# One written list for the slots around each later image's beginning, and 1/std turned on VectorE

## The chip, the cores and the metric

The kernel runs on one core of one Trainium2 chip. The metric is the device time of one execution in microseconds (us), the median over the runs of a kernel. Engines are TensorE (PE, with its weight loads as PEld), VectorE (DVE), ScalarE (ACT), GpSimd (POOL) and SyncE (SP), which issues most of the DMAs. Each has its own queue, in the order in which the program issues; they meet through semaphores.

## The reference, cut to what matters

Four images of 128 channels by 128 x 128 pixels go through two layers, all in float32. Each layer first normalises its input over groups of four channels of an image (`_gn`), so nothing of a layer can start on an image before that image's statistics are complete.

```python
# layer 0: token mixing, per pixel over the 128 channels
def _block(x, ...):
    t = _ln(t, ln0_g, ln0_b)
    y1 = _ln(t, ln1_g, ln1_b)
    t = t + einsum('btc,oc->bto', sigmoid(y1) * y1, W_out)
    y2 = _ln(t, ln2_g, ln2_b)
    wht = einsum('btc,oc->bto', y2, W_whiten)
    k = square(relu(einsum('btc,hc->bth', wht, W_key)))      # 512 hidden
    kv = einsum('bth,ch->btc', k, W_value)
    r = sigmoid(einsum('btc,oc->bto', wht, W_recep))
    return t + r * kv
x = x + block(_gn(x)) + transposed(block(transposed(_gn(x))))   # the same twice
# layer 1: 3x3 convolution, 128 to 128 channels, expert 0 alone, bias,
# and a squeeze-and-excite factor per output channel
v = _gn(x); avg = v.mean(axis=(2, 3))
out = conv3x3(v, weight[0]) + bias_e[0]
x = x + out * sigmoid(relu(avg @ se_w1.T) @ se_w2.T)
```

Both halves of layer 0 work pixel by pixel, so they are the same and are computed once and doubled.

## The kernel before, in words

**Tiles.** An image has 32 chunks of 512 pixels (four rows); two chunks are a pair `g`, so an image has 16 pairs (`NP`) and the run has 64. A block of 16 rows (`NBLK` = 8 per image) stays in SBUF from its load to the store of its result.

**Layer 0 on a pair.** Short words name its operations; a digit in a word is the chunk of the pair, and in `pk`, `re`, `sq` and `kv` a second digit is one of four hidden quarters. ScalarE normalises by group (`u`), TensorE turns the chunk so that pixels lie on partitions (`Tu`), VectorE takes statistics over channels (`bn`), GpSimd makes 1/std and the shift out of them (`nb`, with a power in L642), ScalarE applies them (`t`), GpSimd applies gain and shift (`g`, `b`). A second normalisation (`z1`, its transposes `Tz`), `silu`, the product `att` and the sum `T` follow; then the third statistics (`bn2`, `nb2`).

**1/std of the third normalisation.** It is not applied to the pixels' rows. It is turned, stored and spread: `Tr` (L698) is a TensorE transpose of the 128 x 8 tile `rs` into a bank "rt", `rc` (L702) copies that to SBUF on VectorE, `W` (L706) stores the 8 x 128 rows to DRAM from SyncE, `R` (L711) reads each chunk's 512 values back, spread over 128 partitions, and `cp` (L715) multiplies the turned chunk `tt` with it into `y`, the input of the key products `pk` (L726) and of the receptance `pr` (L744). `re`, `sq`, `kv` (L753), `th`, `q`, `x` and `S` finish the layer; `bx` takes statistics for layer 1.

**Layer 1 on a block.** A transformed (Winograd-like, along the rows) convolution: VectorE makes six mixtures `v0` to `v5` of the rows, TensorE multiplies each with its transformed weights `u` (`c0` to `c5`, three matmuls of some 512 columns each, L791 to L793), and VectorE and ScalarE put the results together (`e1`, `e3`, `a` to `d`, `y0` to `y3`). It runs four slots behind layer 0 and reaches across images without a break.

**Order.** The lists of words are the order of issue, for all engines at once. In the steady part the list ORDER is one slot: slot `s` runs each word `op:k` on pair `s - k`; conv words take turns, even and odd slots doing half a block each. FILL and HANDOVER are lists written out for the first slots and for the stretch where layer 1 of image 0 starts; END is that of the last four slots.

**The two chains.** When an image begins, two chains of small steps have to be run. `input_norm(b)` makes the group statistics of image `b` out of the statistics of its input (`xs`, read from DRAM a second time by SyncE, `fetch` and `in`): an aggregate, two tiny matmuls `pm` (L401) and `pv` (L409), a power on GpSimd. `conv_setup(b)` does the same for layer 1 (L484 to L508), computes the squeeze-and-excite factor by three more matmuls (L512, L518, L521) and two tanh, and scales the six transformed weights with it on VectorE (`scale`, `add_identity`, L535 and L539). It reads the weights anew from DRAM, three of them only when the previous image's last block has used theirs. Both are generators; a `yield` ends a step. In the slots of ORDER a step is run after every third word:

```python
if s % NP == done and b > 1:
    chains.append(conv_setup(b - 1))
...
    if n % 3 == 2:
        for chain in chains:
            next(chain, None)
```

so `input_norm` of an image lies in the slot before the image begins and `conv_setup` in the slot `done` = 3 after it. HANDOVER and END have the steps of `conv_setup` as words of their own, `*`.

Of the kernel before, what the change touches and what calls it, by code (L numbers as in the profile page):

```python
# [13 lines left out]
P = 128  # L14
# [29 lines left out]
    in1:20 u1:4 in0:20 z10:1 g1:2 bn00:3 fetch:21 z11:1 bn01:3 nb2:0 b0:2 Tr:0 Tz10:1 rc:0  # L44
    nb0:3 W:0 silu0:1 Tz11:1 att0:1 silu1:1 in1:21 bn10:2 R0:0 att1:1 in0:21 b1:2 t0:3 T0:1
# [4 lines left out]
    att0:2 sq02:0 pw2:1 sq03:0 kv02:0 T0:2 th0:0 nb2:1 nb1:3 Tr:1 Tz11:2 t1:4 rc:1 kv03:0  # L50
    sq10:0 W:1 pk13:0 q0:0 silu1:2 Tu1:5 in0:23 re12:0 att1:2 bn20:2 t0:4 R0:1 pr1:0 g1:4
    bn01:5 kv10:0 sq11:0 R1:1 x10:0 T1:2 Tu0:5 sq12:0 kv11:0 z10:3 bn00:5 tt1:1 tt0:1 nb0:5
    kv12:0 th1:0 cp0:1 re13:0 pr0:1 sq13:0 cp1:1 pk03:1 z11:3 S1:1 pk00:1 bn21:2 th0:1
    kv13:0 g0:4 S0:1 re00:1 Tz11:3 bx0:0 pk01:1 re03:1 b1:4 sq00:1 silu1:3 pk02:1 b0:4
    bn11:4 re01:1 Tz10:3 att1:3 re02:1 nb2:2 bn10:4 silu0:3 pk12:1 q1:0 pk10:1 re12:1 T1:3
    att0:3 sq03:1 bn21:3 sq01:1 kv00:1 nb1:4 re10:1 Tr:2 pk11:1 sq02:1 rc:2 sq10:1 W:2
    pk13:1 re11:1 T0:3 kv01:1 sq11:1 bn20:3 t1:5 kv02:1 x11:0 R0:2 kv03:1 sq12:1 nb2:3 tt0:2
    q0:1 re13:1 R1:2 pr1:1 bx1:0 t0:5 kv10:1 S0:2 kv11:1 sq13:1 kv12:1 x10:1 z10:4 cp0:2
    tt1:2 pk01:2 g0:5 S1:2 th1:1 pk00:2 cp1:2 re01:2 g1:5 Tr:3 pk03:2 re00:2 rc:3 kv13:1
    sq00:2 re03:2 in1:23 pk02:2 q1:1 pk10:2 bx0:1 x11:1 kv00:2 Tz10:4 bx1:1  # L60
# [11 lines left out]
    x10:4 cp1:3 Tr:2 pk02:3 rc:2 q1:4 bx0:4 t1:0 x11:4 g1:0 z10:1 bx1:4 pk10:3 kv00:3 Tz10:1  # L72
    g0:0 re03:3
# [13 lines left out]
    Tu1:18 kv12:13 re01:14 pk12:14 bn01:18 re03:14 Tu0:18 u0:19 pk02:14 bn00:18 g0:17 Tr:15  # L87
# [10 lines left out]
    Tr:16 att0:17 rc:16 x10:15 bn11:18 W:16 pk12:15 re11:15 bx1:13 tt0:16 nb1:18 sq11:15  # L98
    pk13:15 T0:17 u0:20 bx0:15 t1:19 R0:16 Tu0:20 bn20:17 kv10:15 kv11:15 R1:16 re12:15
    S0:16 re13:15 att1:17 bn00:20 g0:19 sq12:15 sq13:15 kv12:15 g1:19 * kv13:15 cp0:16 u1:20  # L100
    * b1:19 u1:21 Tu1:20 q1:15 pk01:16 z10:18 bn01:20 x11:15 pk00:16 nb0:20 re01:16 bx1:15
    Tz10:18 pr0:16 re00:16 T1:17 sq00:16 * tt1:16 silu0:18 bn21:17 * th0:16 att0:18 sq01:16
    cp1:16 nb2:17 t0:20 * pk10:16 p:0 bn11:19 pk11:16 t1:20 pk03:16 S1:16 * T0:18 b0:19
    Tr:17 re10:16 kv00:16 * rc:17 re03:16 in0:32 kv01:16 W:17 g1:20 re11:16 bn10:19 Tu1:21
    z11:18 pk02:16 b1:20 bn01:21 pk12:16 R0:17 re02:16 nb1:19 * Tz11:18 bn11:20 sq02:16
    tt0:17 u0:21 kv02:16 fetch:33 S0:17 sq03:16 bn20:18 * Tu0:21 re12:16 R1:17 pk13:16 *
    sq10:16 bn00:21 kv03:16 g0:20 silu1:18 cp0:17 pr1:16 z11:19 q0:16 b0:20 att1:18 sq11:16
    kv10:16 * T1:18 sq12:16 nb0:21 tt1:17 * in0:33 re13:16 kv11:16 in1:33 th1:16 pk00:17
    S1:17 fetch:34 sq13:16 * z10:19 kv12:16 * bn10:20 * * re00:17 kv13:16 bn21:18 nb1:20 *
    Tz10:19 * t0:21 cp1:17 pk01:17 in0:34 Tz11:19 pk02:17 re01:17 * * silu1:19 pk10:17 * q:0  # L110
    silu0:19 nb2:18 pr0:17 q2:0 sq00:17 att1:19 * re10:17 att0:19 t1:21 T1:19 pk03:17 q1:16
    x10:16 Tr:18 sq01:17 kv00:17 rc:18 bn21:19 re02:17 W:18 g1:21 kv01:17 sq02:17 T0:19
    pk12:17 th0:17 g0:21 in1:34 re03:17 kv02:17 bn20:19 x11:16 R0:18 sq03:17 tt0:18 z10:20
    pk11:17 S0:18 b0:21 kv03:17 * bx0:16 sq10:17 pk13:17 nb2:19 q0:17 re12:17 Tz10:20 *
    re11:17 kv10:17 z11:20 cp0:18 pr1:17 * pk00:18 * sq11:17 b1:21 bn10:21 Tz11:20 re13:17
    kv11:17 silu0:20 p2:0 pk02:18 re00:18 v3:0 Tr:19 silu1:20 pk01:18 v1:0 th1:17 rc:19
    att1:20 bn11:21 W:19 re02:18 att0:20 * re01:18 nb1:21 T1:20 c1:0 sq01:18 bn21:20 u0:22
    R1:19 T0:20 u1:22 bn20:20 R0:19 tt0:19 e1:0 Tu1:22 tt1:18 x10:17 sq02:18 bn01:22 c3:0
    R1:18 z11:21 nb2:20 * fetch:35 sq13:17 sq12:17 Tu0:22 pr0:18 sq00:18 bn00:22 e3:0
    pk03:18 th0:18 v4:0 nb0:22 kv12:17 * cp1:18 kv13:17 re03:18 cp0:19 pk11:18 q1:17 pk10:18  # L120
    in0:35 re11:18 in1:35 c4:0 re10:18 x11:17 fetch:36 t1:22 v0a:0 sq10:18 kv00:18 g1:22 c:0
    sq03:18 kv01:18 S1:18 t0:22 S0:19 pk12:18 d:0 pk13:18 g0:22 re12:18 in0:36 kv02:18
    z10:21 * kv03:18 b1:22 in1:36 sq11:18 pr1:18 fetch:37 q0:18 sq12:18 Tz10:21 bx1:16
    x10:18 re13:18 kv10:18 th1:18 pk00:19 v5a:0 silu0:21 Tz11:21 re00:19 v2:0 pk01:19
    silu1:21 q:1 kv11:18 b0:22 sq13:18 att1:21 re01:19 tt1:19 sq00:19 T1:21 c2:0 in0:37
    in1:37 bn21:21 pk03:19 S1:19 Tr:20 kv12:18 cp1:19 re03:19 rc:20 kv13:18 a:0 W:20 pk10:19
    q1:18 pk11:19 x11:18 re10:19 att0:21 sq01:19 R0:20 re11:19 pk12:19 T0:21 sq10:19 R1:20
    pk02:19 bn20:21 re12:19 kv00:19 v5b:0 nb2:21 fetch:38 kv01:19 v0b:0 re02:19 bn10:22
    pr0:19 sq02:19 sq11:19 kv02:19 th0:19 tt0:20 sq03:19 pr1:19 cp0:20 sq12:19 pk13:19 S0:20
    th1:19 b:0 tt1:20 re13:19 kv03:19 bx0:17 pk02:20 q0:19 tt0:21 bn11:22 x10:19 re02:20  # L130
    pk00:20 sq13:19 cp1:20 kv10:19 nb1:22 * pk03:20 re00:20 S1:20 kv11:19 S0:21 y1:0 sq00:20
    kv12:19 bx1:18 pk10:20 d8:0 c5:0 bx1:17 re03:20 sq02:20 kv13:19 sq03:20 re10:20 pk11:20
    q1:19 pk01:20 y2:0 re11:20 in0:38 x11:19 kv00:20 re01:20 pr0:20 sq11:20 ca:0 sq01:20
    pk12:20 y3:0 z10:22 p:1 kv01:20 in1:38 Tr:21 kv02:20 th0:20 rc:21 W:21 kv03:20 re12:20
    c0:0 sq10:20 q0:20 x10:20 R0:21 bx0:20 pk13:20 R1:21 bx0:19 kv10:20 re13:20 pr1:20
    sq12:20 fetch:39 sq13:20 kv11:20 th1:20 cp0:21 kv12:20 y0:0 kv13:20 q1:20 pk00:21 bx1:19
    in1:39 in0:39 bx0:18
# [9 lines left out]
    y0:-5 cp1:5 pk02:5 u0:2 c5:-5 sq03:5 bx1:6 Tr:4 re02:5 S1:5 g1:3 b1:3 rc:4 y3:-5 b0:3  # L147
    bn11:3 bn10:3 kv01:5 Tu1:2 sq02:5 pk10:5 nb1:3 bn01:2 re10:5 Tu0:2 sq10:5 pk11:5 q:-4
    v1:-4 W:4 pk13:5 kv02:5 tt0:4 re11:5 pr1:5 re13:5 kv03:5 th1:5 c1:-4 z10:3 bn00:2 z11:3
    v2:-4 R0:4 Tz10:3 q0:5 cp0:4 q2:-4 pk12:5 silu0:3 nb0:2 pk00:4 re12:5 x10:5 e1:-4 v5a:-4  # L150
    v3:-4 S0:4 R1:4 v0a:-4 t1:2 t0:2 v0b:-4 g1:2 kv10:5 att0:3 Tz11:3 T0:3 pr0:4 g0:2 sq11:5
    silu1:3 re00:4 load c3:-4 sq13:5 sq12:5 kv11:5 u1:1 att1:3 b0:2 bn10:2 sq00:4 pk02:4
    b1:2 kv12:5 bn11:2 tt1:4 kv13:5 nb1:2 T1:3 e3:-4 Tu1:1 c2:-4 u0:1 th0:4 re02:4 S1:4
    bn21:3 bn20:3 u0:0 q1:5 a:-4 z10:2 b:-4 pk01:4 cp1:4 Tu0:1 pk03:4 kv00:4 bx0:5 re01:4
    nb2:3 pk10:4 Tr:3 v4:-4 c4:-4 re03:4 re10:4 sq10:4 z11:2 bn00:1 sq01:4 v5b:-4 Tz10:2
    pk12:4 silu0:2 sq02:4 sq03:4 bn01:1 rc:3 Tz11:2 kv01:4 c:-4 d:-4 pk11:4 kv02:4 re12:4
    tt0:3 u1:0 pk13:4 W:3 R0:3 y2:-4 x11:5 ca:-4 nb0:1 sq12:4 kv03:4 S0:3 y1:-4 t1:1 silu1:2
    g1:1 b1:1 R1:3 re13:4 q0:4 c0:-4 att0:2 cp0:3 bn11:1 t0:1 re11:4 sq11:4 att1:2 T0:2 T1:2
    Tu0:0 pr1:4 kv10:4 g0:1 p:-3 bn21:2 pk02:3 th1:4 pk00:3 b0:1 bn20:2 sq13:4 x10:4 nb2:2
    re00:3 q:-3 re02:3 kv11:4 Tu1:0 kv12:4 bn10:1 pk01:3 pr0:3 y0:-4 nb1:1 tt1:3 re01:3  # L160
    cp1:3 th0:3 S1:3 sq01:3 bn01:0 p2:-3 q2:-3 kv13:4 Tr:2 pk03:3 pk11:3 d8:-4 rc:2 sq02:3
    sq00:3 bn00:0 re03:3 nb0:0 W:2 z10:1 c5:-4 q1:4 pk13:3 tt0:2 re11:3 pk10:3 v1:-3 S0:2
    kv00:3 y3:-4 v3:-3 kv01:3 v0a:-3 re13:3 re10:3 x11:4 pr1:3 z11:1 kv02:3 pk12:3 R0:2 t1:0
    c1:-3 th1:3 re12:3 cp0:2 g1:0 Tz10:1 pk00:2 sq11:3 pk01:2 Tz11:1 sq03:3 v4:-3 kv03:3
    silu0:1 q0:3 sq10:3 R1:2 e1:-3 v2:-3 t0:0 silu1:1 att0:1 re00:2 v0b:-3 g0:0 c3:-3 b1:0
    tt1:2 T0:1 att1:1 pk02:2 kv10:3 bn20:1 sq13:3 S1:2 kv11:3 e3:-3 re01:2 sq12:3 re02:2
    T1:1 bn11:0 b0:0 sq01:2 kv12:3 kv13:3 bn21:1 pk03:2 re03:2 sq03:2 sq02:2 x10:3 bn10:0
# [47 lines left out]
def conv_preact_kernel(  # L215
# [863 lines left out]
```

## Time and profile before

| | |
|---|---|
| median of 3 runs | 1893.07 us (1892.37 to 1893.11) |
| profiled execution | 1896.06 us, span 1894.3 us, mean granted TensorE clock 0.993 |
| busy in the span | TensorE 1818.5 us, VectorE 1353.5, ScalarE 1276.4, GpSimd 1158.6 |
| `pk` L726 and `kv` L753 | 1024 matmul records each, mean 598 and 593 ns |
| `rt` L698 | 64 matmuls, 64 weight loads |
| `rrow` L702 | 64 copies on VectorE, mean 275 ns |
| `rs` L642, the power on GpSimd | 192, mean 1650 ns |
| `rd` stores L706, `R` loads L711 | 64 of 4 KB, 128 of 256 KB (spread) |

A float32 matmul leaves two records where its columns are streamed twice, a transpose one. Matmuls are pipelined: the duration of a record is longer than the step from its start to the start of the next, and the step is what TensorE's time is made of. A wait line names who waited, for whom, the total in us, how often, and the longest. A timeline line gives start and length in us, the engine, the line, and in brackets the idle time before it with what ended it.

### The profile page before, as it was taken

What the parts mean: (1) busy time and instruction counts of PE and PEld (TensorE: products, weight loads), DVE (VectorE), ACT (ScalarE), POOL (GpSimd) and SP (SyncE); (2) the same over time, 40 slices, a digit from 0 to 9 for tenths busy, and PEclk for the clock granted to TensorE, in tenths of its full rate; (3) what the DMA queues carried; (4) which work ended last, traced back from release to release, by engine and by line L of the source; (5) the groups of instructions that cost most, each with busy time, mean ns of one, the idle gap of its engine ahead of it and who ended that gap; (6) DMA issues with size and microseconds to landing.
All of it is one profiled execution on the core that took longest, in us unless ns stands there. A gap on an engine that the chain in (4) does not pass through costs nothing.

```text
span 1894.3 us, 21662 instructions
## 1 busy us (share of the span) xinstructions
PE 1818.5 (96%) x6160; PEld 946.7 (50%) x6160; DVE 1353.5 (71%) x3336; ACT 1276.4 (67%) x2493; POOL 1158.6 (61%) x1915
## 2 busy tenths in 40 slices
PE   3799999999999999998999999999999999999998
PEld 2555555555445555544555555455455555544443
DVE  6767766677667677777677777667676667666987
ACT  2889898898567776766677767776677777753000
POOL 2878878887366666665676666666566677641211
PEclk9899999999999999999999999999999999999999
DMA  6211112121211221212212211112111111111112
GB/s 226 79 46 56 53 48 92 67 70 57 90 55 67 90 77 69 101 54 83 89 67 90 89 46 68 67 57 79 46 45 67 67 56 67 49 38 43 52 67 89
DMA packets 41031, 133.54 MB, mean 70 GB/s; under 512 B 5048, under 2 KB 9935, under 8 KB 32847
## 3 DMA queue, kind: packets, MB, share of 16 engines
q1 hardware_dynamic: 40464, 131.76, 19.8%
q8 instruction: 49, 0.80, 0.2%
q14 instruction: 72, 0.58, 0.1%
q10 hardware_dynamic: 446, 0.40, 0.1%
HBM read 97.14 MB, written 35.00 MB: 70 GB/s over the span
## 4 chain that ended last, share of the span: by engine, by line
PE 85%; DVE 4%; ACT 3%; POOL 3%; issue 1%; POOLq 0%; DVEq 0%; ACTq 0%
PE pk L726 21%; PE kv L753 21%; PE m L791 8%; PE m L792 8%; PE m L793 8%; PE pr L744 5%; PE att L687 5%; PE tt L588 3%; PE z1t L588 2%; PE ut L588 2%; POOL rs L642 1%; ACT t L595 1%; DVE st L619 1%; ACT z L595 1%; ACT h L730 1%
## 5 line engine op out<-in xcount | busy, mean ns | idle before, releaser
L726 PE MATMUL pk<-y,wk_s 128*128 128x512 f32 x1024 | 503.1, 598 | 7.0 <-DVE y L715 5.6
L753 PE MATMUL kv<-h,wv 128*128 128x512 f32 x1024 | 487.0, 593 | 0.0
L730 ACT ACTIVATE h<-pk,kbias 128x512 f32<-128x512 f32 x512 | 350.1, 687 | 172.9 <-PE pk L726 166.4
L642 POOL TENSOR_TENSOR rs<-rs,nhalf 128x8 f32<-128x8 f32 x192 | 316.8, 1650 | 11.7 <-DVE rs L635 6.0
L753 PEld LDWEIGHTS kv<-h,wv 128*128 128x128 f32 x1024 | 186.0, 190 | 208.0 <-issue 185.7
L736 ACT ACTIVATE h<-h 128x512 f32<-128x512 f32 x480 | 284.4, 629 | 4.2
L726 PEld LDWEIGHTS pk<-y,wk_s 128*128 128x128 f32 x1024 | 183.2, 191 | 197.0 <-issue 147.1
L773 POOL TENSOR_TENSOR x<-x,r 128x512 f32<-128x512 f32 x128 | 165.2, 1291 | 188.1 <-DVE r L769 178.6
L595 ACT ACTIVATE t<-ut,nb,rs 128x128 f32<-128x128 f32 x512 | 192.0, 465 | 125.6 <-POOL nb L649 117.7
L619 DVE BATCH_NORM_STATS2 st<-t 128x6 f32<-128x128 f32 x1024 | 219.4, 276 | 22.4 <-POOL t L670 20.0
L595 ACT ACTIVATE z<-t,nb,rs 128x128 f32<-128x128 f32 x512 | 210.1, 488 | 12.7 <-POOL nb L649 12.2
L666 POOL TENSOR_TENSOR t<-t,g 128x512 f32<-128x512 f32 x128 | 163.3, 1281 | 74.2 <-ACT t L595 73.9
L791 PE MATMUL m<-v,u 128*128 128x512 f32 x384 | 199.2, 600 | 6.3 <-ACT e L867 3.5
L792 PE MATMUL m<-v,u 128*128 128x508 f32 x384 | 195.7, 591 | 0.0
L793 PE MATMUL m<-v,u 128*128 128x508 f32 x384 | 195.3, 590 | 0.0
L631 POOL TENSOR_TENSOR rs<-st 128x8 f32<-128x8 f32 x186 | 57.8, 311 | 215.2 <-DVE st L619 213.7
L670 POOL TENSOR_TENSOR t<-t,b 128x512 f32<-128x512 f32 x128 | 163.8, 1285 | 6.7
L687 PEld LDWEIGHTS att<-wo,y 128*128 128x128 f32 x1024 | 131.5, 196 | 26.4 <-issue 17.6
L619 DVE BATCH_NORM_STATS2 st<-ut 128x6 f32<-128x128 f32 x512 | 112.3, 283 | 42.2 <-PE ut L588 42.2
L748 ACT ACTIVATE r<-pr,rbias 128x512 f32<-128x512 f32 x128 | 87.7, 685 | 79.8 <-PE pr L744 58.0
L687 PE MATMUL att<-wo,y 128*128 128x128 f32 x1024 | 138.9, 281 | 2.4 <-ACT y L681 1.8
L744 PE MATMUL pr<-y,wr_s 128*128 128x512 f32 x256 | 131.5, 596 | 3.2 <-ACT h L730 2.5
(155 smaller groups left out, 2441.0 us busy)
## 6 DMA issues: line engine op xcount, KB each, us to landing
R<-rd SPq DMA_DIRECT2D x128, 256.0 KB
out<-x SPq DMA_DIRECT2D x32, 1024.0 KB
x<-in_x SPq DMA_DIRECT2D x31, 1024.0 KB
xs<-in_x SPq DMA_DIRECT2D x48, 512.0 KB
u<-raw SPq DMA_DIRECT2D x18, 192.0 KB
raw<-u SPq DMA_DIRECT2D x6, 192.0 KB
x<-in_x SPq DMA_DIRECT2D x2, 512.0 KB
rd<-rrow SPq DMA_DIRECT2D x64, 4.0 KB
```

What stands on the lines that cost most here:

```text
L595: nc.scalar.activation(dst[:, s, :], src[:, s, :], AF.Identity, bias=nb[:, i : i + 1], scale=rs[:, i : i + 1],)
L619: nc.vector.bn_stats(st[:, h * SUB + s, :], src[:, s, :])
L642: nc.gpsimd.tensor_tensor(rs, rs, nhalf, ALU.pow)
L687: nc.tensor.matmul(att[:, ts(s, P)], y[:, ts(s, P)], wo, start=True, stop=True)
L726: nc.tensor.matmul(pk, wk_s[:, ts(j, P)], S["y2", g, h], start=True, stop=True)
L730: nc.scalar.activation(k, S["pk", g, h, j], AF.Relu, bias=kbias[:, j : j + 1])
L736: nc.scalar.activation(k, k, AF.Square)
L744: nc.tensor.matmul(pr, wr_s, S["y2", g, h], start=True, stop=True)
L753: nc.tensor.matmul(S["kv", g, h], wv[:, j, :], S.pop(("h", g, h, j)), start=(j == 0), stop=(j == NH - 1))
L791: nc.tensor.matmul(pc, u[:, 1], v, start=True, stop=False)
L792: nc.tensor.matmul(pc[:, :, 1:W], u[:, 0], v[:, :, 0 : W - 1], start=False, stop=False)
L793: nc.tensor.matmul(pc[:, :, 0 : W - 1], u[:, 2], v[:, :, 1:W], start=False, stop=True)
```

## The change

**1/std.** `Tr` and the bank "rt" go; `rc` now does the turning on VectorE. For the third normalisation `norm_start` uses one tile of four 8-column parts per pair, of which 1/std is the first. The transpose is used square by square of 32 x 32: of the 128 x 32 tile, 1/std comes out in the first 8 rows of each of four stacks of 32 rows, so `W` becomes four stores, each of 8 rows by 32 columns. The word `Tr` is taken out of every list.

```diff
-        rs, nb, sm = term("rs"), term("nb"), term("sm")
-        eng.tensor_tensor(rs, st[:, :, 1], st[:, :, 4], ALU.subtract)
-        eng.tensor_tensor(rs, rs, rs, ALU.mult)
-        eng.tensor_scalar(rs, rs, C / 4, C * LN_EPS, ALU.mult, ALU.add)
+        if k < 2:
+            rs, nb, sm = term("rs"), term("nb"), term("sm")
+            d, dd = rs, rs
+        else:
+            S["turn", g] = four = small.tile([P, 4, N], F32, tag="four", name="four", bufs=2)
+            rs, nb, sm, dd, d = four[:, 0], None, four[:, 1], four[:, 2], four[:, 3]
+        eng.tensor_tensor(d, st[:, :, 1], st[:, :, 4], ALU.subtract)
+        eng.tensor_tensor(dd, d, d, ALU.mult)
+        eng.tensor_scalar(dd, dd, C / 4, C * LN_EPS, ALU.mult, ALU.add)
         eng.tensor_tensor(sm, st[:, :, 2], st[:, :, 5], ALU.add)
-        eng.tensor_tensor(rs, rs, sm, ALU.add)
+        eng.tensor_tensor(rs, dd, sm, ALU.add)
...
     def turn_std(g):
-        rs, _ = S.pop(("norm", 2, g))
-        S["rt", g] = rt = bank("tr", "rt")
-        nc.tensor.transpose(rt[:N, :P], rs, ident)
-
-    def copy_std(g):
-        S["rrow", g] = row = small.tile([N, P], F32, tag="rrow", name="rrow", bufs=1)
-        nc.vector.tensor_copy(row, S.pop(("rt", g))[:N, :P])
+        S.pop(("norm", 2, g))
+        four = S.pop(("turn", g)).rearrange("p a n -> p (a n)")
+        S["rrow", g] = rows = small.tile([P, 4 * N], F32, tag="rrow", name="rrow", bufs=2)
+        nc.vector.transpose(rows, four)
 
     def store_std(g):
         S["rd", g] = rd = dram.tile([N, P], F32, tag="rd", name="rd")
-        nc.sync.dma_start(rd, S.pop(("rrow", g)))
+        rows = S.pop(("rrow", g))
+        for a in range(0, P, 32):
+            nc.sync.dma_start(rd[:, a : a + 32], rows[a : a + N, :])
```

**The list.** BOUND takes the place of eight runs of ORDER around the beginnings of images 2 and 3: the slot before and the seven slots from it (`BOUND_SLOTS` = 1, 7). Its numbers count from the image: pairs from its first pair, blocks from the first block of the image before it, whose convolution is then beginning, and reads from the first pair of the next image. `*` is a step of `conv_setup`, `+` one of `input_norm`. Among its 838 words are 35 `*` and 7 `+`. Here are its beginning, the stretch with most of the chain, and its end:

```diff
+BOUND_SLOTS = 1, 7
+BOUND = """
+    p2:-3 q2:-3 fetch:0 v3:-3 x11:-4 * u0:-1 u1:-1 load Tu0:-1 z11:-2 Tu1:-1 re00:-3 Tz10:-2
+    pk01:-3 v1:-3 * bn00:-1 bn01:-1 v0a:-3 v4:-3 c3:-3 + * sq00:-3 Tz11:-2 silu0:-2 re01:-3
+    att0:-2 silu1:-2 v2:-3 in0:0 nb0:-1 e3:-3 att1:-2 t0:-1 + T0:-2 g0:-1 c1:-3 + e1:-3
+    tt1:-3 b0:-1 bn20:-2 T1:-2 + cp1:-3 t1:-1 pk03:-3 re03:-3 + in1:0 sq03:-3 bn21:-2
+    bn10:-1 c2:-3 + g1:-1 pk10:-3 + kv00:-3 pk02:-3 u0:0 a:-3 Tu0:0 b1:-1 b:-3 u0:1 p:-2
...
+    x10:0 tt1:1 bx1:-1 nb1:4 y0:-1 cp1:1 re00:1 nb2:2 S1:1 kv11:0 kv12:0 bx1:-2 pk10:1 *
+    sq00:1 c5:-1 kv13:0 z10:3 d8:-1 re10:1 pk03:1 Tz10:3 z10:4 pk12:1 bn01:5 re03:1 * y3:-1
+    bn00:5 sq01:1 silu0:3 in0:5 att1:3 re12:1 q1:0 rc:2 in1:5 * * * kv00:1 z11:4 sq03:1
+    kv01:1 pr0:1 v2:0 * W:2 v1:0 att0:3 load th0:1 * T1:3 kv02:1 nb0:5 t0:5 x11:0 pk11:1
+    T0:3 * bn20:3 kv03:1 sq10:1 pk13:1 re11:1 sq11:1 * bn21:3 * * tt1:2 g0:5 nb2:3 * R0:2
+    re13:1 tt0:2 * q0:1 * * kv10:1 cp0:2 * u0:6 t1:5 * * fetch:6 pk00:2 * re00:2 kv11:1
+    pk02:2 * S0:2 c1:0 * * g1:5 v3:0 * * R1:2 pr1:1 re02:2 b0:5 * pk01:2 * rc:3 e1:0 S1:2
+    c3:0 u1:6 * sq13:1 b1:5 sq12:1 kv12:1 * W:3 x10:1 th1:1 kv13:1 re01:2 cp1:2 e3:0 Tu0:6
...
+    cp1:4 x11:3 th0:4 d8:0 bx1:3 pk10:4 pk11:4 re10:4 kv02:4 pk13:4 re11:4 nb2:5 in1:7
+    sq10:4 rc:5 sq11:4 W:5 kv03:4 R0:5 pr1:4 q0:4 re13:4 pk12:4 kv10:4 sq13:4 R1:5 re12:4
+    y3:0 kv11:4 x10:4 sq12:4 S0:5 kv12:4 bx0:4 th1:4 cp0:5 kv13:4 pk00:5 q1:4
+"""
```

**Around it.** `slot` keeps one chain, `input_norm(1)`, in the last slot but one of image 0, a step after every eleventh word; `group_norm` gets one more `yield`, between the sum with GN_EPS and the power. The reads of the next image's pairs that BOUND names are taken out of what ORDER's slots distribute.

```diff
-        chains = []
-        b = s // NP
-        if s == (b + 1) * NP - (2 if b == 0 else 1) and b + 1 < B:
-            chains.append(input_norm(b + 1))
-        if s % NP == done and b > 1:
-            chains.append(conv_setup(b - 1))
+        chain = input_norm(1) if s == NP - 2 else iter(())
...
-            if n % 3 == 2:
-                for chain in chains:
-                    next(chain, None)
+            if n % 11 == 4:
+                next(chain, None)
...
-        for s in range(ORDER_FROM, B * NP - END_SLOTS):
+        work_off(handover, conv_setup(0), None, same, same, same)
+        done = ORDER_FROM
+        for b in range(2, B):
+            for s in range(done, b * NP - before):
+                slot(s, order)
+            work_off(
+                bound, conv_setup(b - 1), input_norm(b), lambda n: (b - 1) * NBLK + n,
+                lambda n: b * NP + n, lambda n: (b + 1) * NP + n,
+            )
+            done = b * NP + beyond
+        for s in range(done, B * NP - END_SLOTS):
             slot(s, order)
```

## The prediction

> **What bounds the kernel now.** I read the page first, then TensorE's windows, its waits, and the timelines around single instructions. The page says that TensorE is busy nearly all the time, and no other engine is near it:
>
> ```profile
> PE 1818.5 (96%) x6160; PEld 946.7 (50%) x6160; DVE 1353.5 (71%) x3336; ACT 1276.4 (67%) x2493; POOL 1158.6 (61%) x1915
> ```
>
> An average hides the places where it is not so. I cut the span at the `rt` transposes (L698), of which each pair of chunks has one; between two of them lies one slot of the written order. The first row is a slot in the middle of an image, the next four lie around the beginning of image 2, the last three around that of image 3. Columns: the length, then busy time of each engine, the granted clock, the DMA share:
>
> ```profile
> 593.20:621.00 27.80, 27.80 (x97) 14.41 (x96) 21.98 (x55) 18.99 (x37) 16.18 (x29) 1.00 0.11 38
> 732.20:762.40 30.20, 28.51 (x101) 14.94 (x100) 19.18 (x51) 21.35 (x42) 20.01 (x33) 1.00 0.25 87
> 790.10:818.40 28.30, 27.91 (x96) 14.40 (x95) 19.96 (x48) 21.27 (x42) 20.30 (x32) 1.00 0.37 131
> 846.20:878.40 32.20, 29.62 (x106) 15.47 (x105) 21.89 (x56) 21.79 (x44) 20.68 (x33) 1.00 0.36 128
> 878.40:910.80 32.40, 29.60 (x96) 15.80 (x95) 26.43 (x66) 19.17 (x37) 17.10 (x29) 0.95 0.13 40
> 1188.80:1219.00 30.20, 28.50 (x101) 14.93 (x100) 19.32 (x50) 21.36 (x42) 20.04 (x33) 1.00 0.25 88
> 1302.30:1336.20 33.90, 31.32 (x106) 16.76 (x105) 20.83 (x53) 21.94 (x44) 21.30 (x33) 0.95 0.30 107
> 1336.20:1368.60 32.40, 29.59 (x96) 15.60 (x95) 25.64 (x64) 19.10 (x37) 16.88 (x29) 0.95 0.08 23
> ```
>
> The ordinary slot is 27.80 us of TensorE without a hole (its neighbour, 621.0 to 648.8, too). So what leaves TensorE's queue there is gained in full, and work of another engine is worth nothing. The others are longer by 2.4 + 0.5 + 4.4 + 4.6 = 11.9 us at image 2, and by 2.4 + 6.1 + 4.6 = 13.1 us at image 3: 25.0 us above the ordinary slot. TensorE's waits between 846 and 911 us say where in the second half of it:
>
> ```profile
> PE pk L726 <- DVE y L715: 2.8, 1, 2.8
> PE pm L487 <- ACT r L748: 2.0, 1, 2.0
> PE p L521 <- ACT row L524: 0.4, 1, 0.4
> PE pk L726 <- ACT se L527: 0.3, 1, 0.3
> ```
>
> From 732 to 762 it waits 1.2 us at the bank after `pm` and 0.5 us at a product. Each is a step of `input_norm` or `conv_setup`, or stands behind one: `pm` waits for the last use of an "h" bank, `pk` for a `y` that stands in VectorE's queue behind the `scale` and `add_identity` steps (VectorE is 26.43 us busy in that slot, 21.98 in the ordinary one).
>
> **Part 1, 1/std turned on VectorE.** Out of TensorE's queue go 64 transposes:
>
> ```profile
> L698 PE MATMUL rt<-ident,rs x64: 272/273/377, 64.8 to 1703.1; 128*8 128x128 f32 x64
> 621.00 0.27 PE L698 MATMUL rt<-ident,rs 128*8 128x128 f32 x1
> 621.10 1.02 PE L753 MATMUL kv<-h,wv 128*128 128x512 f32 x2
> ```
>
> The 0.27 us is the time through the pipeline; what counts is from its start to that of the next matmul, 0.10 to 0.11 us (four 128-column transposes elsewhere take 0.44). 64 x 0.109 = **7.0 us**; nearly all lie in stretches where TensorE has no hole. TensorE also no longer waits for `rs` at `rt`: its waits list 1.8 us at the first pair and 0.7 us near 409 us. What follows may be late itself (at the first pair it next waits 1.4 us for `u`), so of the bounds 0 and 2.5 I take 1.2 us.
>
> VectorE loses 64 copies of 0.275 us and gets 64 turns of 128x32. No row shows a turn: the 128x1 copies (0.147) and the copy just named are the nearest rows, I take 0.2. Either way it is under 0.1 us per slot on an engine with 6 us idle there: nothing. Its wait changes from `rt` to GpSimd's `rs`. In the ordinary odd slot `rs` ends at 676.05 and VectorE reaches `rc` at 676.91, in the even one it has 4 us; so the instructions queued behind (`bn`, `v`) wait no longer than now. GpSimd's five steps per pair stay five. The "tr" bank of `rt` comes free: nothing while TensorE is not waiting for it.
>
> SyncE gets 192 more stores, 4 instead of 1 per pair at 0.285 us of issue: 0.86 us more before the two `R` loads, which wait for all four, and before the `xs` and image loads queued behind. SyncE mostly waits (733 us for `rrow` in all), so its own time costs nothing; what matters is when `R` lands. In the even slot `R` is issued at 651.67 and used at 659.79: covered by several us. The odd slot is the tight one:
>
> ```profile
> 675.86 0.34 SPq L894 DMA_DIRECT2D out<-x  x1
> 677.21 0.28 SPq L706 DMA_DIRECT2D rd<-rrow  x1
> 680.47 0.80 SPq L711 DMA_DIRECT2D R<-rd  x2
> 684.03 0.69 DVE L715 TENSOR_TENSOR y<-tt,R 128x512 f32<-128x512 f32 x1 [0.94 <-DMA R<-rd]
> ```
>
> There 3.26 us pass from store to load, against 1.24 in the even slot: the store stands behind the 1 MB of `out`, issued just before. Four small stores behind the same 1 MB should land with it, so I expect 0 to 0.9 us later. `y` ends at 684.71 and its `pk` starts at 685.73: 1.0 us cover that. Cost: 0.
>
> **A rule against this.** Each row of `rd` is now written as four pieces of 128 bytes, not one of 512. The Trainium skill (DMA: Bandwidth & Descriptors, Specifications) says that below 512 bytes a DMA does a read-modify-write and falls short of the line rate. No row shows such a store. If it doubles the 1.24 us, `R` is 0.86 + 1.24 = 2.1 us later, 1.1 us more than is covered, in the 19 odd pairs from 23 to 59: 21 us lost. By the 3.26 us row the wait is for the queue ahead, not for the 4 KB. I take the row, and keep 21 us for a rival.
>
> **Part 2, the list.** It holds the same TensorE work as eight slots (I count 8 x 27.6 us of it), but places each step of the chains. What stays are their own matmuls, 14 records per image at some 0.11 us (`pm` starts at 860.89, two of them are through at 861.11): 1.5 us. What should go:
> - `fetch` of weights 4, 0, 5 comes over 60 us of TensorE work after the last products that free their buffers; near 851 us SyncE stood at them and their issues for 26.9 us. The `load` and `xs` words stay at about one per slot.
> - From `bn_aggr` to the first product of the new image, `c1:0`, lie some 18 us of TensorE work. The chain's own steps there add up to 7 or 8 us (1.01 for the aggregate, 0.95 for `avg`, 0.61 and 0.37 for scaling, the rest 0.15 to 0.8 each).
> - From the aggregate to the last `scale` the chain now takes some 70 us of the order instead of 34 (858 to 892), so that VectorE's share of its 35 steps does not push back `y`.
>
> What is left of waits I size by HANDOVER, a list of the same kind around image 1: 363.5 to 537.6 us is 174.10 us with 169.14 busy, so 5.0 us of holes. Of these 2.1 is at the conv's very first product and 0.7 at `rt`, neither of which recurs: 2.2 us are left. I take 2.2 per image, 0 and 7 as ends (7 is HANDOVER's holes times 1.4, the ratio in which image 2's 10.4 us above its own matmuls stand to its 7.5 us of waits). Gain: 25.0 - 2 x 1.5 - 2 x 2.2 = **17.6 us**.
>
> **A rule that sizes part 2.** The hole of 2.80 us is followed by slow matmuls:
>
> ```profile
> 893.10 1.33 PE L726 MATMUL pk<-y,wk_s 128*128 128x512 f32 x2 [2.80 <-DVE y L715]
> 894.23 1.06 PE L588 MATMUL ut<-ident,u 128*128 128x128 f32 x4
> 895.08 1.06 PE L588 MATMUL z1t<-ident,z 128*128 128x128 f32 x4
> ```
>
> Four transposes take 0.85 us from start to start, twice the 0.44, and the clock column reads 0.95; the slot is 4.6 us longer, not 2.8. The Trainium skill (TensorE: Matmul & The Clock Gate, Part 1: The HAM clock gate) halves the clock only after an idle window of some 3.4 us. By the rule alone 2.80 us would cost 2.80; with both images the gain would be 3.6 us less. I take the row: the holes that go are worth their slow wake, and a new hole of that size would cost the same.
>
> **Part 3, image 1.** `input_norm(1)` stays in its slot but steps every eleventh operation. Slot 279.1 to 300.7 is 21.60 us, its neighbour 20.00; own matmuls some 0.4, so 0 to 1.2, taken 0.6.
>
> **Sum.** 7.0 + 1.2 + 17.6 + 0.6 = 26.4 us. The profiled execution took 1896.06 us (span 1894.3), 3 us above the median 1893.07; the parts come from it and are taken off the median: **1866.7 us**.
>
> **Rivals.**
> - *The list waits as much as HANDOVER* (7 us per image), the small terms give nothing: 7.0 + 25.0 - 3.0 - 14.0 = 15 us, 1878. For: one order of six FIFO queues has to fit. Against: the conv is already running here, and HANDOVER also builds the weights. 0.14.
> - *The waits at the boundaries don't go*, the chain's latency only moves: part 1 alone, 1885. Against: 18 us against 8. 0.05.
> - *Slower*: the odd slots' store. If `R` lands more than 1.0 us later, `pk` waits in 19 slots, by the excess each. At 2.1 us it eats 21 of the 26 us; the change is slower overall by more than 0.2% once it is some 2.6 us late, sooner where the hole wakes the clock slowly: 1897 or more. For: the 0.94 us wait that `y` already has there. Against: the 1 MB in front. 0.04.
> - My forecast has 0.77.
>
> **How the numbers follow.** A measurement of this kernel can tell about 0.2%, some 4 us, from no change. Best end: no waits in the list (+4.4), all of 2.5 and 1.2 (+1.9), and 1 us for what I cannot see: 1859. Worst end taken in: the HANDOVER case with 1 to 2 us off part 1, 1880. Outside lie 1885 and 1897 and tails of my own case, some 0.15. Faster: 0.77 + 0.14 + 0.05 less a little, 0.95; slower 0.04; between 0.01.
>
> **What would show it.** Ordinary slots of 27.69 us; slots around images 2 and 3 near 28.5 with no wait over 1 us on `pm`, `pk` or a product; odd slots in which `y` waits for `R` 1 us or less and `pk` never waits for `y`. Wrong, if the ordinary odd slot is longer than 27.8, if the list shows a hole of 2 us or a clock of 0.95, or if the gain is under 14 us.

## The result, and the profile after

The changed kernel takes 1872.68 us (median of 4 runs, 1870.81 to 1874.61) against 1892.72 us (4 runs, 1889.78 to 1893.11) for the kernel before on the same chip: a ratio of 0.9898, 95% interval 0.988 to 0.9915. A second set gave 1873.14 us (4 runs, 1869.52 to 1874.85), 0.9889 [0.9875, 0.9903]. So the gain is 20 us where 26.4 were forecast; the forecast of 1866.7 is 6 us too low, inside its range. The profiled execution took 1870.88 us, span 1868.9.

The page's line of engines, to be read against the one in the prediction: TensorE has 64 records less and 15.5 us less of busy time. The span fell by 25.4 us, so some 10 us of the gain were idle time.

```profile
PE 1803.0 (96%) x6096; PEld 940.6 (50%) x6096; DVE 1346.3 (72%) x3336; ACT 1271.1 (68%) x2493; POOL 1163.7 (62%) x1915
```

Without `rt` I cut the span at every eighth `z1` transpose (a slot of the order, but shifted against the `rt` cuts). The rows are the windows of the changed kernel: an odd and an even ordinary slot, then nine slots around the beginning of image 2 and nine around that of image 3, then the `input_norm(1)` slot. Columns as before: length, busy time of each engine, granted clock, DMA share.

```profile
991.77:1016.76 24.99, 24.99 (x90) 13.34 (x89) 17.27 (x44) 19.16 (x38) 17.84 (x31) 1.00 0.28 102
961.39:991.77 30.38, 30.38 (x102) 15.46 (x101) 22.57 (x55) 20.58 (x41) 18.54 (x31) 1.00 0.27 88
709.30:961.39 252.09, 248.52 (x856) 129.99 (x855) 189.46 (x466) 179.68 (x354) 167.14 (x273) 1.00 0.23 78
1157.91:1410.41 252.50, 248.80 (x856) 129.85 (x855) 181.24 (x450) 179.69 (x354) 170.17 (x273) 1.00 0.18 62
278.73:299.26 20.53, 20.53 (x82) 11.59 (x81) 14.36 (x44) 18.04 (x37) 16.91 (x32) 1.00 0.25 79
```

Cut in the same way, the kernel before has 25.10 and 30.50 us for the ordinary slots, 259.40 and 260.80 for the two stretches of nine and 21.57 for the last row. The ordinary slot lost its 0.11 us. The stretches lost 7.3 and 8.3 us, 1.0 of each through `rt`. Nine ordinary slots are 246.5 us (five odd, four even), so 5.6 and 6.0 us are left above them.

TensorE's waits in the two stretches of the changed kernel (engine, line, what for, total, times, longest):

```profile
PE m L863 <- DVE v L887: 1.6, 1, 1.6
PE m L863 <- ACT h L808: 0.8, 1, 0.8
PE pk L798 <- DVE y L787: 0.7, 1, 0.7
PE ut L656 <- ACT t L663: 0.5, 1, 0.5
...
PE m L863 <- DVE rrow L772: 1.0, 1, 1.0
```

The 2.8 us on `pk`, the 2.0 on `pm` and the 1.2 on `pr` are gone. What remains are shorter waits on products of the convolution (`m`), on one `pk` and on one `u` turn; image 3 shows the same (1.6, 1.0, 0.5, 0.4, 0.2 us), its 1.0 being the last line.

The new turn costs VectorE 0.2 us a pair, and its own wait is short (group row: busy, mean ns, idle before it and its releaser):

```profile
L772 DVE STREAM_TRANSPOSE rrow<-four 128x32 f32<-128x32 f32 x64 | 12.8, 201 | 9.3 <-POOL four L715 9.2
```

The odd slot, from the timeline of the changed kernel:

```profile
613.45 2.12 SPq L778 DMA_DIRECT2D rd<-rrow  x4
617.68 0.82 SPq L783 DMA_DIRECT2D R<-rd  x2
621.40 0.69 DVE L787 TENSOR_TENSOR y<-tt,R 128x512 f32<-128x512 f32 x1 [2.08 <-DMA R<-rd]
622.14 1.13 PE L798 MATMUL pk<-y,wk_s 128*128 128x512 f32 x2
```

Behind the 1 MB of `out` the four stores take 2.12 us to issue, not 4 x 0.285, and `R` follows 4.23 us after the first of them (3.46 us before, for the same pair). `y` then waits 2.08 us and ends just ahead of its `pk`: the cover of 1.0 us is used up, TensorE stands for 0.02 us here. Over the run `y` waits 23.3 us for `R` (13.8 before), but `pk` stands for it only three times, for 0.02, 0.69 and 0.23 us.

### The profile page after: what moved, and what is told of

Read it like the earlier page. It is cut to its first block, busy times and chain, and to the rows that moved or that the text cites. A ratio compares the mean times of both kernels' runs of the same rounds, so it can differ in the third digit from the quotient of the medians.

```text
span 1868.9 us, 21819 instructions
## 1 busy us (share of the span) xinstructions
PE 1803.0 (96%) x6096; PEld 940.6 (50%) x6096; DVE 1346.3 (72%) x3336; ACT 1271.1 (68%) x2493; POOL 1163.7 (62%) x1915
## 4 chain that ended last, share of the span: by engine, by line
PE 85%; POOL 4%; DVE 3%; ACT 3%; issue 1%; DMA 1%; SPq 0%; DVEq 0%; POOLq 0%
PE kv L825 22%; PE pk L798 21%; PE m L863 8%; PE m L865 8%; PE m L864 8%; PE pr L816 5%; PE att L760 5%; PE tt L656 3%; PE z1t L656 3%; PE ut L656 2%; POOL rs L715 1%; ACT t L663 1%; DVE st L687 1%; POOL t L739 1%; POOL t L743 1%
## 5 line engine op out<-in xcount | busy, mean ns | idle before, releaser
L825 PE MATMUL kv<-h,wv 128*128 128x512 f32 x1024 | 492.7, 593 | 0.0
L715 POOL TENSOR_TENSOR rs<-rs,nhalf 128x8 f32<-128x8 f32 x128 | 215.2, 1681 | 6.0 <-DVE rs L708 6.0
L739 POOL TENSOR_TENSOR t<-t,g 128x512 f32<-128x512 f32 x128 | 163.9, 1287 | 74.9 <-ACT t L663 74.5
L841 DVE SCALAR_TENSOR_TENSOR r<-r,kv 128x512 f32<-128x512 f32 x128 | 86.9, 679 | 86.8 <-PE kv L825 84.0
L764 DVE TENSOR_TENSOR t<-att,t 128x512 f32<-128x512 f32 x128 | 87.6, 685 | 79.7 <-PE att L760 79.2
```

The costliest lines, as they stand in the source:

```text
L715: nc.gpsimd.tensor_tensor(rs, rs, nhalf, ALU.pow)
L825: nc.tensor.matmul(S["kv", g, h], wv[:, j, :], S.pop(("h", g, h, j)), start=(j == 0), stop=(j == NH - 1))
```

## The experiments

All are set against the kernel before on the same chip. "Slot 22" below is the first ordinary slot after HANDOVER (510 to 543 us after the change).

The change once more, beside the first of these kernels:

> The changed kernel once more, beside the others of this call: some 1871 to 1875 us; both theories read the others against it.

Measured: the second set of the section above.

**One part at a time.** First the turn alone: `Tr` out of every list, `rc` on VectorE with four stores, the rest as before.

```diff
-    re10:2 c2:1 in1:0 a:1 pk12:2 sq01:2 sq10:2 Tr:1 v0a:1 sq02:2 re03:2 sq03:2 re12:2 b:1
+    re10:2 c2:1 in1:0 a:1 pk12:2 sq01:2 sq10:2 v0a:1 sq02:2 re03:2 sq03:2 re12:2 b:1
```

> The kernel before with 1/std turned on VectorE and four stores, its lists and chains otherwise as they were. My theory: ordinary slots of 27.69 us (64 x 0.109 = 7.0 us), and 2 to 3 us more because TensorE no longer waits for rs at rt: 9 to 10 us less than before, some 1883 us. Rival (the late R eats it): pk waits for y in many odd slots, 3 to 5 us less than before at most, 1888.

Measured: 1889.58 us (11 runs), 0.9979 [0.997, 0.9987], 4 us faster and not 9 to 10. The ordinary slots lost their 0.11 us as expected. Of the 2 to 3 us expected where TensorE no longer waits at `rt`, 0.8 came (near 410 us). And the ten slots around the beginning of image 2 (742.6 to 1032.5 us before) got 2.0 us longer, 289.8 to 291.9, in spite of 1.1 us less of `rt`. TensorE's waits there were

```profile
PE pk L729 <- DVE y L718: 3.2, 2, 2.8
PE pm L486 <- DVE mv L483: 2.0, 1, 2.0
PE m L794 <- ACT e L870: 1.6, 2, 1.0
```

against 2.8, 2.0 and 0.9 before. Of the 3.1 us lost there (2.0, and the 1.1 that `rt` should have given), 1.7 are not the work of `R`: the wait on `pm` is as long as before (1.95 us), but the granted clock behind it is 0.50 from 854.4 to 857.8 us, which the kernel before has around image 3 alone (more on this below). The other 1.4 us, and 0.6 us around image 3, come with the later `R`: a second `pk` waits for a `y` that waits for `R` (2.44 us), and a product waits longer, though no run shows that `R` is what delays the product. So the later `R` is not free where VectorE is crowded. By the profile 7.0 + 0.8 - 2.0 = 5.8 us are gained; the interval of the runs is 2.5 to 5.7.

Then the list alone, with `rt` on TensorE as before, once with `rt` just ahead of `rc` (first kernel) and once placed where `rs` has ended (second). In the slots of BOUND `rt` takes a bank of the tag "h":

```diff
+        S["rt", g] = rt = bank("h" if (g + 2) % NP < 8 and g >= 2 * NP - 2 else "tr", "rt")
+        nc.tensor.transpose(rt[:N, :P], rs, ident)
```

> The changed kernel with 1/std turned on TensorE as before: rt just ahead of rc in the list BOUND (in an h bank there, since a tr bank would close a circle of waits), the other lists as before. My theory: two boundaries at some 7 us less each, and the chain of image 1 at 1 us less: 14 to 16 us less than before, some 1878 us. If the first holes of the list (0.7 us at pk, 1.6 us at c3) come from the late R and not from the list, they are gone or under 0.5 us here, with one store per pair; if they are the list's own they stay.

> The list with 1/std turned on TensorE once more, but rt placed in the list where TensorE came after GpSimd's rs had ended in the trace of the changed kernel, rc and W behind it (an h bank there). Theory: the list alone is worth 13 to 15 us; what made the first such kernel slow were the places of rt, where TensorE waited for rs: now 1878 to 1882 us, and at the first mark of each list no hole at pk. Rival (the list only works with VectorE's turn, since an extra h bank and an extra copy upset it): 1888 us or more.

Measured: 1902.89 us, 1.0046 [1.0033, 1.006], and 1894.62 us, 1.0011 [1.0003, 1.0019]. The list alone gains nothing. The waits of TensorE over the stretch around image 2, of the first and then of the second kernel:

```profile
PE rt L767 <- ACT h L799: 3.6, 3, 3.1
PE rt L767 <- ACT r L817: 2.4, 2, 1.5
PE ut L657 <- ACT t L664: 1.3, 1, 1.3
```

```profile
PE pk L796 <- ACT h L800: 1.6, 3, 0.8
PE pk L796 <- DVE rrow L772: 1.3, 1, 1.3
PE rt L768 <- ACT r L818: 1.0, 1, 1.0
```

`rt` waits for a bank, or takes one that `pk` or `pr` then waits for. At the beginning of the list, with one store per pair, no `pk` waits in either kernel and the first product waits 0.93 us; after the change these waits are 0.69 and 1.58 us, so that much of them is the later `R`. The sum of the parts (-4 and +1 to +9) is not the change (-20): this list has no room for `rt`. That is a statement on the list with a borrowed bank; the list with `rt` in a bank of its own was not tried: the tags of the order use all eight banks, and in "tr" the order closes to a circle of waits.

**What `R` costs.** Here the store of a finished stack is held back until `R` is issued. The stores of the last two blocks of image 2 (two of 32) are left out in this kernel.

```diff
         if S.get(("rows", k)) == 4:
...
+            if ending:
+                store_block(k)
+            else:
+                held.append(k)
```

> The changed kernel, but SyncE issues the 1 MB store of a finished block behind the next R load of a second chunk (or ahead of the next block's load), no longer ahead of the four small stores. Theory: the small stores and R no longer stand behind the 1 MB; in the odd slots the time from first store to R falls from 3.5 to 5.2 us to about 2.3, y no longer waits for R, the hole at pk before each list goes and that at c3 shrinks: 2 to 4 us less than the changed kernel, 1869 to 1871, and runs closer together than 1870.8 and 1874.6. Rival (the holes are the list's own): within 0.5 us of the changed kernel.

Measured: 1871.7 us, 0.9882 [0.9868, 0.9897]: 1 us below the changed kernel, within its spread. The same place of the timeline as above:

```profile
614.65 1.30 SPq L781 DMA_DIRECT2D rd<-rrow  x4
617.20 0.97 SPq L786 DMA_DIRECT2D R<-rd  x2
620.83 0.69 DVE L793 TENSOR_TENSOR y<-tt,R 128x512 f32<-128x512 f32 x1 [0.32 <-DMA R<-rd]
```

From store to load it is now 2.2 to 2.6 us in odd slots and `y` hardly waits. But the held stores go out later inside the list: there two `R`s come 5.8 and 6.1 us after their store, `pk` starts 1.2 and 1.0 us late behind VectorE, and what the first half of the list gained goes. The other direction, each store split again (eight per pair):

```diff
-            nc.sync.dma_start(rd[:, a : a + 32], rows[a : a + N, :])
+            for n in range(0, N, N // 2):
+                nc.sync.dma_start(
+                    rd[n : n + N // 2, a : a + 32], rows[a + n : a + n + N // 2, :]
+                )
```

> The changed kernel with eight stores of 4 x 32 per pair in place of four of 8 x 32: four more issues of some 0.29 us. If issue time on SyncE is what delays R: R is 1.2 us later, which is past the 0.06 to 1.1 us that pk has left in the odd slots, so pk waits 0.5 to 1.2 us in some 15 to 19 of them: 10 to 20 us more than the changed kernel, 1883 to 1893. If R's time is set by the 1 MB ahead of it, and by nothing that SyncE issues: as the changed kernel, within 1 us.

Measured: 1873.23 us, 0.9893 [0.9878, 0.9907], no slower than the changed kernel. Even slots now take 3.2 us from store to load, odd ones 4.0 to 5.0, and `y` waits up to 2.75 us; `pk` stands for 0.69, 0.16 and 0.34 us in three odd slots. So the expected 10 us and more did not come: the store-to-load time grew by under a microsecond, most of it in slots with cover to spare.

**What is left in the list.** The wait of 0.77 us (1.0 at image 3) on `m` is put down to `h` in one image and to `rrow` in the other. Neither fits: `c3:0` reads the third weight stack, whose `add_identity` ended at 893.22 us, and `c3:0` began at 893.37. The test scales it before the second:

```diff
-        for i in (2, 3):
+        for i in (3, 2):
```

> The changed kernel, conv_setup scaling the weights u3 before u2 (the lists use c1, c3, c2). Theory: the hole ahead of c3:0 in each list (0.77 and 0.96 us, 0.9 and 1.1 us of TensorE's time with the slow wake) is the wait for the last scale and add_identity on VectorE, so it goes: slots at 856 and 1305 us of 42.4 in place of 43.4 us, 2 us less in all. Rival (it waits for ScalarE or for rrow, as the profile names them): the holes stay, no gain.

Measured: 1872.63 us, 0.9889 [0.9876, 0.9902]. The two slots with that wait went from 43.33 and 43.53 us to 42.33 and 42.32, so it was the weights; the 2 us do not show in the median, where the runs differ by as much through other slots (slot 22 has 34.2 us in this run and 32.5 in the profile of the change, the slot at 65 us has 20.1 and 18.5). Three moves together, the third being `c3:-3` placed one TensorE word later because it waits 1.6 us for `v`:

```diff
-    pk01:-3 v1:-3 * bn00:-1 bn01:-1 v0a:-3 v4:-3 c3:-3 + * sq00:-3 Tz11:-2 silu0:-2 re01:-3
+    pk01:-3 v1:-3 * bn00:-1 bn01:-1 v0a:-3 v4:-3 + * sq00:-3 Tz11:-2 c3:-3 silu0:-2 re01:-3
```

> The changed kernel with u3 scaled first, the block stores issued behind R (all blocks stored), and the word c3:-3 of the list moved one TensorE word later, behind Tz11:-2. Theory: all three early holes shrink (c3:-3 by 0.4 of 1.5 us, c3:0 by 0.9, pk by 0.7): 3 to 5 us less than the changed kernel, 1867 to 1870. Rival (the time goes to the next wait in the queue): within 1 us of it.

Measured: 1873.85 us, 0.9895 [0.988, 0.9909]: nothing. Around image 2 the wait moved on to the next words:

```profile
PE ut L659 <- ACT t L666: 2.3, 1, 2.3
PE pk L804 <- DVE row L600: 1.3, 1, 1.3
```

**The two together, where they are safe.** The first kernel has the weight order and a move of `c3:0` in HANDOVER; the second also holds stores back, but only in ordinary slots.

```diff
-    bn20:20 R0:19 tt0:19 e1:0 Tu1:22 tt1:18 x10:17 sq02:18 bn01:22 c3:0 R1:18 z11:21 nb2:20
-    * fetch:35 sq13:17 sq12:17 Tu0:22 pr0:18 sq00:18 bn00:22 e3:0 pk03:18 th0:18 v4:0 nb0:22
+    bn20:20 R0:19 tt0:19 e1:0 Tu1:22 tt1:18 x10:17 sq02:18 bn01:22 R1:18 z11:21 nb2:20
+    * fetch:35 sq13:17 sq12:17 Tu0:22 pr0:18 c3:0 sq00:18 bn00:22 e3:0 pk03:18 th0:18 v4:0 nb0:22
...
+            if k % NBLK in (0, 5, 6, 7) or ending:
+                store_block(k)
+            else:
+                held.append(k)
```

> Two edits to the changed kernel: the third weight stack of the next 3x3 layer is scaled before the second (as in e5, where the slot at the second and third boundary became 42.33 instead of 43.33 us), and in the slot list the first tap c3:0 of the next layer's matmuls moves behind the pair's u and projection matmuls (Tu0:22 pr0:18), so that at image 1 too it stands later than the scale it reads. Theory (TensorE's wait at c3:0 is for the scaled weights alone): the 2.07 us hole near 522 us falls below 0.8, the slot there, which is 32.5 us in some runs and 34.2 in others, stays at 32.5 or below, and the two 1.0 us holes are gone: -2.0 -1.3, and the runs lie closer together; about 1869 against 1872.7. Rival (the wait moves to the next word that needs VectorE or ScalarE): 1872 to 1873, with a hole of over 1 us elsewhere in the same slots.

> As e9, and the four stores of a stack are issued behind the R transfer of the pair, not ahead of it, in ordinary slots only (not in the slots around an image's beginning; in the last image they are issued at once). Theory: W to R in odd slots goes from 3.5-5.2 to about 2.3 us, y waits for R by no more than 0.5 us, and the holes of 0.16 to 0.69 us in front of pk where pairs join go: up to 1 us below e9. Rival (R's lateness is covered by pk's own slack): the time of e9 within 0.5 us.

Measured: 1869.7 us, 0.9871 [0.9854, 0.9887], and 1867.28 us (4 runs, 1865.09 to 1867.96), 0.9858 [0.9844, 0.9873]. The second is faster than the change and than the first; its slowest run is below the fastest of the eight runs of the change and of the four of the first. Its two stretches of nine slots, and TensorE's waits in that of image 2:

```profile
710.40:960.00 249.60, 248.15 (x857) 130.26 (x856) 190.26 (x466) 179.76 (x354) 167.29 (x273) 1.00 0.24 79
1156.40:1406.60 250.20, 248.40 (x857) 130.10 (x856) 181.39 (x450) 179.79 (x354) 170.13 (x273) 1.00 0.18 62
```

```profile
PE m L869 <- DVE v L900: 0.9, 1, 0.9
PE ut L659 <- ACT t L666: 0.5, 1, 0.5
```

2.5 and 2.3 us less than after the change: 1.0 and 1.2 by the weights, 1.5 and 1.1 by `R`. The move of `c3:0` did nothing that the profile shows: the wait of 2.07 us at 522 us stayed, since it stands in slot 22, the first of ORDER, not at that word. ScalarE gets to `e` late there, behind a `t` that waited 5.15 us for GpSimd's `nb`. I had named the wrong place. The first kernel's median is 2.9 us below that with the weight order alone (1872.63), and where these lie is not shown. Nor is the size of the gain by `R` firm around image 2: there the second set's profile of the change has no `pk` wait either (58.6 us for two slots, as in the last kernel, against 60.2 in the first).

**Two engines at once.** In the 6 us ahead of `c3:0` VectorE is slow. From the timelines of the changed kernel:

```profile
885.19 0.62 DVE L603 SCALAR_TENSOR_TENSOR u<-u,rs,row 128x384 f32<-128x384 f32 x1
...
887.37 1.75 DVE L887 SCALAR_TENSOR_TENSOR v<-q,p 128x512 f32<-128x512 f32 x1
889.05 1.35 DVE L607 SCALAR_TENSOR_TENSOR u<-ident,u 128x128 f32<-128x128 f32 x1
890.32 1.63 DVE L603 SCALAR_TENSOR_TENSOR u<-u,rs,row 128x384 f32<-128x384 f32 x1
...
887.12 1.45 POOL L739 TENSOR_TENSOR t<-t,g 128x512 f32<-128x512 f32 x1 [2.05 <-ACT t L663]
888.53 2.99 POOL L743 TENSOR_TENSOR t<-t,b 128x512 f32<-128x512 f32 x2
```

The same `scale` takes 0.62 us while GpSimd is idle and 1.63 while it works. A kernel of its own measures that:

```diff
+            if pool:
+                nc.gpsimd.tensor_tensor(r, h, b, ALU.mult)
+            if dve == "sbuf":
+                nc.vector.scalar_tensor_tensor(o, w, 2.0, a, ALU.mult, ALU.add)
+            elif dve == "psum":
+                nc.vector.tensor_tensor(o, bank, w, ALU.add)
+            elif dve == "one":
+                nc.vector.tensor_scalar(o, w, 1.0, 0.5, ALU.add, ALU.mult)
```

> Not the computation of the reference: seven stretches of 12 equal 128x512 float32 operations, on VectorE, GpSimd or both at once, each beginning when both engines are done with the one before: (0) VectorE with two operands in SBUF, alone; (1) GpSimd's product alone; (2) both; (3) VectorE with one operand in PSUM, alone; (4) that with GpSimd; (5) VectorE with one SBUF operand, alone; (6) that with GpSimd. The output is the last tile, written everywhere. Question: whether the four operations of 1.24 to 1.75 us in the slot of the third 3x3 weight stack, instead of 0.29 to 0.72, come from GpSimd working at the same time. Theory: the operations with two SBUF operands go from about 0.7 us to 1.2 or more in stretch 2, GpSimd's from 1.28 to about 1.5; those with one operand in PSUM stay at about 0.7. Rival (something else of that slot): stretch 2 stays within 10% of stretch 0.

VectorE's stretches of twelve, each kind alone and then with GpSimd (timeline):

```profile
8.96 9.62 DVE L65 SCALAR_TENSOR_TENSOR o<-w,a 128x512 f32<-128x512 f32 x12
41.03 19.97 DVE L65 SCALAR_TENSOR_TENSOR o<-w,a 128x512 f32<-128x512 f32 x12
64.72 8.67 DVE L67 TENSOR_TENSOR o<-bank,w 128x512 f32<-128x512 f32 x12
76.06 8.67 DVE L67 TENSOR_TENSOR o<-bank,w 128x512 f32<-128x512 f32 x12
95.86 6.44 DVE L69 TENSOR_SCALAR o<-w 128x512 f32<-128x512 f32 x12
104.98 16.78 DVE L69 TENSOR_SCALAR o<-w 128x512 f32<-128x512 f32 x12
```

Two SBUF operands: 0.80 us an operation alone, 1.66 with GpSimd, whose own twelve go from 16.00 to 19.92 us. One operand in PSUM: no effect on either. One SBUF operand: 0.54 to 1.40 us. The theory held, and the last pair went beyond it.

## Why the prediction was right, and where it was not

The direction, the order of size and the places were right; the size was 6 us too high. By its own steps, from the two profiles:

- **Part 1, 7.0 us: right.** 0.11 us in the ordinary slots, with and without the list. The small terms came to 1.7 us, not 1.8 (1.2 and 0.6): 0.8 around 410 us, where TensorE no longer waits at `rt`, and 0.9 in the `input_norm(1)` slot. The wait at the first pair gave nothing. The first three slots did get 1.5 us shorter beyond their `rt`, but by a stretch at half rate (74.7 to 78.1 us) that the profile before has and that of the change has not. Like against like: with that stretch they take 47.4 and 47.7 us where `rt` is kept (before; the second kernel with the list alone) and 47.2 to 47.4 where it is gone, without it 46.0 and 45.6 to 46.4.
- **Part 2, 17.6 us: mis-sized, 13.6** (6.3 and 7.3 beyond `rt`). The step that failed is "I take 2.2 per image" for what is left of waits, borrowed from HANDOVER. It is 4.1 and 4.5 us (5.6 and 6.0 less the 1.5 of own matmuls). Two causes are shown: 1.0 to 1.2 us per image at `c3:0` are the order of the last two scaled stacks, and about as much is `R`'s lateness at the beginning of the list, around image 3 in both profiles of the change, around image 2 in the first alone. Counting the slow wake was right: of the 13.6 us, waits make 7.5 (7.6 and 7.2 us before, 3.6 and 3.7 after) and three stretches at half rate, of which none is left, 5.1. With both causes changed, 1.6 and 2.2 are left, the size that was forecast. The prediction also sized `scale` by a row that holds while GpSimd is idle; what that alone adds at `c3:0` was not separated.
- **"Cost: 0" for the store: nearly.** From store to load, odd slots took 0.2 to 1.4 us longer in mid-image, in part more than the 0.9 that was allowed, and 1.8 and 2.5 us longer in the slots where the list begins (0.8 in the second profile around image 2); the cover of 1.0 us was used up. In mid-image that costs next to nothing. In the crowded slots it is not zero: up to 1.4 and 0.6 us around images 2 and 3 with the turn alone, about 1 us per image with the list. The forecasts that `y` waits 1 us or less and that no product does more fell (up to 2.75 and 1.6 us). The 21 us that doubling the store-to-load time would have cost did not come, nor with eight stores. The rule of the Trainium skill (DMA: Bandwidth & Descriptors, Specifications), a read-modify-write below 512 bytes, may still be in the 0.2 us by which a store in four pieces takes longer than its extra issue; the issue behind `out` was the larger term (2.12 us, not 1.14).
- **The slow wake.** The row against the rule (Trainium skill, TensorE: Matmul & The Clock Gate, Part 1: The HAM clock gate) was the better guide, but the price is not fixed: it is 1.7 us or nothing. The same wait of 2.07 us at 522 us is followed by matmuls at full rate in the profile of the change and at half rate in the kernel with only the weights and `c3:0` moved:

```profile
522.13 1.12 PE L863 MATMUL m<-v,u 128*128 128x512 f32 x2 [2.07 <-ACT e L939]
523.09 1.01 PE L864 MATMUL m<-v,u 128*128 128x508 f32 x2
...
523.41 1.98 PE L863 MATMUL m<-v,u 128*128 128x512 f32 x2 [2.07 <-ACT e L939]
525.18 1.90 PE L864 MATMUL m<-v,u 128*128 128x508 f32 x2
```

  32.5 and 34.2 us for the slot. The traces show what decides it. In each of them the granted clock changes only at the edges of a grid of 3.41 us; the page calls this a free-running window. A wait of some 2 us that lies whole between two edges is followed by a clock of 0.50 up to the edge after; one that an edge cuts well inside is not. The kernel before has both within one execution. Its wait of 1.95 us on `pm` is cut into 0.81 and 1.14 us around image 2 (first three rows, one stretch of the grid each; idle is the length less the first busy time) and whole around image 3 (last two rows; the clock stands before the last two columns):

```profile
856.34:859.75 3.41, 2.60 (x18) 1.83 (x16) 2.94 (x11) 3.38 (x8) 2.22 (x4) 1.00 0.68 257
859.75:863.16 3.41, 2.27 (x13) 1.79 (x14) 3.31 (x10) 1.04 (x2) 3.11 (x7) 1.00 0.01 4
863.16:866.58 3.42, 3.42 (x14) 1.78 (x13) 2.67 (x8) 2.08 (x5) 1.80 (x3) 1.00 0.00 0
1313.73:1317.14 3.41, 1.46 (x8) 0.72 (x7) 3.41 (x9) 3.18 (x6) 2.00 (x8) 1.00 0.05 18
1317.14:1320.55 3.41, 3.41 (x12) 2.74 (x13) 2.40 (x9) 1.14 (x4) 2.16 (x3) 0.50 0.00 0
```

  The wait at 522 us is cut into 0.44 and 1.63 us in the profile of the change and whole in the other. Over the twelve traces of the computation, from 80 us on, all 17 stretches of the grid in which TensorE idles for 1.95 us or more are followed by 0.50, none of the 66 with 1.0 to 1.7 us, and 3 of the 7 in between. The page asks for an idle window of some 3.4 us; the measurement decides. So for a hole of some 2 us it is chance whether it costs 1.7 us more.
- **The base.** The parts were measured in an execution 3 us above its median and taken off the median. The two profiled executions differ by 25.2 us, the medians by 20.0: the first profile lies 3.3 us above its median, the second 1.8 below. The profile before has two stretches at half rate, at 75 us and in slot 22, that the second, by where the grid fell, has not: 1.5 and 1.7 us of these 5.1. Where the other 1.9 lie in the unprofiled runs is open. Against the profiles, the working is 26.4 forecast, 22.0 found (7.0 + 1.7 + 13.6, less 0.3 for `R` outside the list), and 3.2 of chance.
- **The rivals.** The list did not wait as HANDOVER does (4.1 to 4.5 us per image, not 7), the boundaries' long waits did go, and the odd slots' store did not cost 20 us. What no rival named is that the two parts need each other: alone they gain 4 us and nothing.

## What to carry to other kernels

An order written out by hand is a packing for one set of operations: before pricing a part of a change by itself, ask whether the other part frees a bank or a queue place that it lives on. A cover of 1 us counts once, and here it was smallest where the changed stretch begins, so price a later transfer there and not in the steady slot. When a residue is borrowed from a similar stretch, ask which engines overlap in the new one: an operation's row holds for the company it was measured in. Before two profiles are set against each other, count the stretches at half rate in each: here two of them were 3.2 us of luck.

## What the runs showed of the hardware

- VectorE is held up by GpSimd on SBUF operands: from 0.80 to 1.66 us (two operands), from 0.54 to 1.40 us (one SBUF operand), no change with one operand in PSUM. The Trainium skill (SBUF — State Buffer, SBUF: two separate sides) describes a shared port pair that is held for a whole instruction; twelve pairs took 19.97 us where one after the other they would have taken 9.62 + 16.00 = 25.6, so some of it still overlapped.
- TensorE's granted clock falls to 0.50 for one stretch of a grid of 3.41 us, 1.7 us lost, when TensorE idled for 1.95 us or more within the stretch before (17 of 17). An edge of the grid can save a longer hole: one of 3.25 us, cut into 1.88 and 1.36 us (1287 us, the first kernel with the list alone), was followed by the full clock.
- Four 1 KB stores behind a 1 MB store took 2.12 us to issue from SyncE, 1.30 us when that store was not ahead of them.
